# A conditional layer on quarters of TensorE, with a value product between its token tiles, and attention contexts by two groups

## The chip, the cores and the metric

The kernel runs on one core of a Trainium2 chip. The metric is the device time of one execution in microseconds (us), the median over runs; less is better. The engines are called PE or TensorE (matrix products), DVE or VectorE, ACT or ScalarE, POOL or GpSimd, and SP or SyncE, which issues most DMA transfers. PSUM is the memory that TensorE writes its results to, in banks of 128 partitions by 512 float32 values. All matrix products here are in float32, and the trace shows two matmul records for each matmul instruction.

## The reference

The input is 64 batches of 64 tokens by 1024 values. A conditional layer mixes the 64 tokens of each batch with a 64x64 matrix chosen by the batch's condition, then comes attention with 32 heads of 32 values over the 64 tokens of a batch, and a residual. A routed layer and a quantised feed-forward layer follow, with another residual; the change does not touch them.

```python
def _L0_cond_ref(x, condition, weights):
    W = weights[condition]                       # 64 x 64 for each batch
    return jnp.einsum('bct,bcd->bdt', x, W)

def _L0_attn_ref(x, attn_qkvw, attn_qkvb, attn_ow, attn_ob):
    ...
    qkv = x @ attn_qkvw + attn_qkvb              # 1024 -> 3 x 1024
    ...
    scores = jnp.einsum('bhqd,bhkd->bhqk', q, k) * scale
    probs = jax.nn.softmax(scores, axis=-1)
    ctx = jnp.einsum('bhqk,bhkd->bhqd', probs, v)
    ctx = jnp.transpose(ctx, (0, 2, 1, 3)).reshape(B, S, H)
    return ctx @ attn_ow + attn_ob

x = x + _L0_attn_ref(_L0_cond_ref(x, itok_B_0_15, L0_cond_weights), ...)
x = x + _L0_ffn_ref(_L0_cond2_ref(x, itok_B_0_7, ...), ...)
```

## The kernel before

The 4096 tokens are worked in eight blocks (`b`) of 512: four token tiles (`j`) of 128 tokens, each two batches. One function, `attention` (L183), does the conditional layer, the projections to queries, keys and values, and the attention up to the contexts; the contexts go to a DRAM buffer `ctx_d`, and a second stage (out projection, routed layer, feed-forward layer) reads them from there in pairs of tiles. The first two pairs' out projections already run at the end of `attention`.

**Seven products for eight.** Every projection is a 2x2 matrix product by the Strassen-Winograd scheme. The weight matrix has quarters A11, A21, A22, A12 and four sums S1 to S4 (`sums`, L269). The tokens (the output of the conditional layer, transposed, so that rows are features) have quarters B11, B21 (tiles 0 and 1) and B12, B22 (tiles 2 and 3) and four sums T1 to T4 (`t_of`, L369; T4 on L366). A job (L378) makes the products in `ORDER` = 1, 6, 7, 5, 2, 4, 3, on four PSUM banks: products 1 and 2 share bank a, 6 has b, 7 and 4 share c, 5 and 3 share d. Product 1 uses A11 and B11, product 2 uses A12 and B21, product 6 uses S2 and T2. After product 1 ScalarE copies bank a (`p1`, L399); products 6 and 7 leave `u6`, `u7` on VectorE (L402); the other four leave results with `put`. `rows_job` (L416) makes queries (`psq`, into `qT`) and keys (`psk`, into `kbd`, L412/L414) for one of four head groups `c`, with products of 1.72 us; `values_job` (L449) makes values (`psv`, into `vbd`, L468/L470) for one of two column groups `g`, with products of 3.43 us.

**Conditional layer.** `conditional` (L337) copies the 64x64 matrices of the two batches of a tile into the diagonal of a zeroed 128x128 matrix `wbd` (L375; on VectorE for block 0, on GpSimd afterwards). Eight products, one for each tile and feature half `hf`, are four matmuls of 128x128 by 128 columns into one PSUM bank each (L350). Each is copied to B by VectorE (tiles 0 and 2, L356) or ScalarE (tiles 1 and 3, L358). Token tiles and their matrices (`x`, `wg`) are loaded one block ahead (`load_x`).

**Planner.** The order of work is made by a small planner with a clock of its own, `now`. `run(cost, product, rest)` (L598) first does all that is due by `now`, then issues the product, then `behind`, which is the rest (evacuations) of the product before, then one store out of `later`, and then adds `cost` to `now`. Work is put at a time with `at`. A `phase` (L612) takes a list of products ("fills") and puts two groups of attention work into it, one at its beginning and one at half its length.

**A group** is two units of (feature half, token half), 16 score rows. Its `begin` (L573) issues the scores on TensorE (L491), then the contexts of every earlier group that is ready (`contexts`, L566), and then plans the rest: maxima, subtraction and exponential (L503, L504, L507), normalising 3.4 later (L513 to L515), splitting into 16-bit planes (L521), the transposing transfer `phT` on SP's queue (L526), and `pT`, the joined transpose (L533), after another 8. A group is ready for its context when both `pT` are made. `context` (L536) issues 16 matmuls (L543) into a bank of the pool `ps_c`; at once afterwards ScalarE makes two copies with the bias, `co` (L553, pool `p2` with two buffers), and issues each one's store to `ctx_d` from its own queue (L554).

**Pools.** PSUM has four banks "g" for products and the conditional layer, two banks for one tile of scores, and two banks "c" for contexts.

**What the changed parts stand beside.** At the end of a block the fills are `conditional(b+1)`, the first values job of block b+1 and its first query and key jobs. In block 0 the sums S1 to S4 of a weight are made when the weight is first loaded, all four in a row: for `q` and `k` after product 4 of a job (fill 5), for the second value weight in fill 4 of phase 0, and for the second query weight in the first values job. In the last phase of the last block the fills are the out projections of the first two pairs (`poa` to `pod`, L1019), and the last contexts are planned at `now + 41`:

```python
fills += op.pair(0) + op.pair(1)
length = 24
at(now + 41, contexts)
```

Of the kernel before, what the change touches and what calls it, by code (L numbers as in the profile page):

```python
# [20 lines left out]
P = 128  # L21
# [161 lines left out]
def attention(tc, a, x_t, ctx_d, ident, dram, ps_g, KC, PB, NBLK, NCH, HPC, H, C, chores, early, op):  # L183
# [27 lines left out]
    with ExitStack() as ctx, ExitStack() as mid:  # L211
# [5 lines left out]
        pTp = pool(ctx, "pT1", 4, side="right")  # L217
        sm = pool(ctx, "sm1", 3, side="right")
        ps_s = pool(ctx, "ps_s", 1, space=PSUM)
# [49 lines left out]
        def sums(eng, at):  # L269
            eng.tensor_tensor(at("S1"), at("A21"), at("A22"), ALU.add)  # L270
            eng.tensor_tensor(at("S2"), at("S1"), at("A11"), ALU.subtract)
            eng.tensor_tensor(at("S3"), at("A11"), at("A21"), ALU.subtract)
            eng.tensor_tensor(at("S4"), at("A12"), at("S2"), ALU.subtract)
# [4 lines left out]
        def load_qk(b, wh, c, eng=None):  # L278
            t = w_qk[b, wh, c] = wp.tile([P, 7, KQ, P], F32, tag="wqk", name=f"w{wh}_{b}_{c}")
            if b == 0:  # L280
                if (wh, c) == ("q", 0):
                    held(t[:, SLOT["A11"], 0, 0:1], x_next[0][1])
                for key in RAW:
                    nc.sync.dma_start(t[:, SLOT[key], :, :], quarter(key, (0 if wh == "q" else H) + c * P, P))
                def rest():
                    sums(eng or nc.vector, lambda key: t[:, SLOT[key], :, :])
                    nc.gpsimd.dma_start(qk_d[wh, c], t)
                return rest
# [6 lines left out]
        def load_v_raw(g, eng):  # L295
# [9 lines left out]
            def rest():  # L305
                sums(eng, at)
                for slot in range(7):
                    later.append(lambda slot=slot: nc.gpsimd.dma_start(v_d[g][:, slot, :, :], w_v[0, g, slot]))
            return rest
# [3 lines left out]
        first_sums = [load_qk(0, "q", 0), load_qk(0, "k", 0, nc.gpsimd)]  # L313
        nc.sync.dma_start(bqkv, a["qkvb_t"])
        first_sums.append(load_v_raw(0, nc.gpsimd))
# [4 lines left out]
        wbd = []  # L320
        for j in range(PB):
            t = w.tile([P, P], F32, tag=f"wbd{j}", name=f"wbd{j}")
            nc.vector.memset(t, 0.0)
            wbd.append(t)
# [12 lines left out]
        def conditional(b, tiles):  # L337

            def one(hf, j):
                key = f"B{hf + 1}{j // 2 + 1}"  # L340
                box = []

                def product():
                    xt = tiles[j][0]
                    if j % 2 == 0:
                        B[key] = yp.tile([P, KQ, HB], F32, tag=key, name=f"y{key}_{b}")
                    ps = ps_g.tile([P, 4, P], F32, tag="g", name=f"cond_{b}_{j}_{hf}")
                    for q in range(KQ):
                        k = hf * KQ + q
                        nc.tensor.matmul(ps[:, q, :], xt[:, k * P:(k + 1) * P], wbd[j], start=True, stop=True)  # L350
                    box.append(ps)

                def rest():
                    dst = B[key][:, :, (j % 2) * P:(j % 2 + 1) * P]
                    if j % 2 == 0:
                        nc.vector.tensor_copy(dst, box[0])  # L356
                    else:
                        nc.scalar.copy(dst, box[0])  # L358
                    if (hf, j) == (0, 3):
                        t_of("T1", "B12", "B11")  # L360
                    elif (hf, j) == (1, 3):
                        t_of("T2", "B22", "T1")
                        t_of("T3", "B22", "B12")
                    elif (hf, j) == (1, 1):
                        B["T4"] = B["B12"]
                        nc.vector.tensor_tensor(B["T4"], B["B21"], B["T2"], ALU.subtract)  # L366
                return 0.95, product, rest
# [5 lines left out]
            for j, (_, wg) in enumerate(tiles):  # L373
                for r in range(2):
                    (nc.gpsimd if b else nc.vector).tensor_copy(wbd[j][halves[r], halves[r]], wg[halves[r], :])  # L375
            return [one(0, j) for j in range(PB)] + [one(1, j) for j in (2, 3, 0, 1)]

        def job(name, cost, n, matmuls, put, begin=None, done=None):  # L378
# [4 lines left out]
            def one(i):  # L383
                def product():
                    if i == ORDER[0] and begin:
                        begin()
                    bank = BANK[i]
# [1287 lines left out]
```

## Time and profile before

| | us |
|---|---|
| median of 3 runs | 2479.53 |
| the 3 runs | 2477.33, 2479.58, 2479.53 |
| the profiled execution, its own time | 2482.55 |
| its span on the core | 2480.8 |
| of the span, start up to the second product of the first query job | 0.00 to 21.34 |
| attention up to the last block's last phase | 21.34 to 1384.53 |
| last phase of attention, with two pairs' out projections | 1384.53 to 1447.71 |
| second stage | 1447.71 to 2480.80 |

The profile is of one execution. Its span is the time from the first to the last instruction on the core; the time of the execution has some 2 us more around it. Busy times by engine, the chain of work that ended last, groups of equal instructions ("out<-in", count, total and mean time, idle time before them with what ended it) and the records themselves can be read. The mean granted TensorE clock over the span is 0.992 of the full one. What keeps TensorE waiting in the four parts, from the table of its busy time by stretch (columns: stretch in us, then busy us and instructions of PE, PEld, DVE, ACT and POOL, granted clock, DMA share, GB/s):

```profile
0.00:21.34 21.34, 10.53 (x73) 9.98 (x73) 11.93 (x28) 4.38 (x8) 5.02 (x12) 1.00 0.84 262
21.34:1384.53 1363.19, 1354.53 (x9724) 1180.68 (x9727) 831.88 (x1586) 545.63 (x821) 181.76 (x324) 1.00 0.69 210
1384.53:1447.71 63.18, 57.24 (x306) 28.13 (x306) 31.91 (x48) 29.65 (x35) 22.76 (x12) 0.95 0.58 172
1447.71:2480.80 1033.09, 1013.43 (x3136) 485.05 (x3135) 649.13 (x1297) 373.97 (x440) 151.23 (x103) 0.99 0.53 140
```

TensorE is busy for nearly all of the second part, which holds the seven hand-overs from one block to the next.

### The profile page before, as it was taken

How to read it: one execution, taken by the hardware profiler on the slowest of the kernel's cores; microseconds unless marked ns; L12 is line 12 of the kernel's file. 1: busy time of each engine (PE TensorE's matmuls, PEld its weight loads, DVE VectorE, ACT ScalarE, POOL GpSimd, SP SyncE). 2: the span in 40 equal slices, each digit the busy share in tenths (PEclk: the TensorE clock that was granted, in tenths of full speed). 3: DMA queues.
4: the chain of work that ended last, by engine and by line, in shares of the span. 5: the costliest groups of instructions: out<-in, count | busy, mean ns of one | idle time of the engine just before them, and what ended most of it. 6: DMA issues, size and time to landing. Idle time of an engine off the chain costs nothing.

```text
span 2480.8 us, 34182 instructions
## 1 busy us (share of the span) xinstructions
PE 2435.7 (98%) x13232; PEld 1703.8 (69%) x13232; DVE 1524.9 (61%) x2957; ACT 953.6 (38%) x1303; POOL 360.8 (15%) x451
## 2 busy tenths in 40 slices
PE   8999999999999999999999999999999999999996
PEld 7888888888888888888888644444454545454452
DVE  4585585675764755745646623333367777778787
ACT  1243353443443533533534533343423333333333
POOL 5010011011122221110000233334200000000001
PEclk9999999999999999999999999999999999999997
DMA  8795767676677667766646668877744443434343
GB/s 281 262 266 153 225 192 232 191 208 203 205 201 246 206 188 248 201 202 181 171 145 215 187 213 248 271 232 239 227 151 79 87 79 81 85 73 91 71 96 70
DMA packets 417980, 446.76 MB, mean 180 GB/s; under 512 B 299665, under 2 KB 353938, under 8 KB 404114
## 3 DMA queue, kind: packets, MB, share of 16 engines
q1 hardware_dynamic: 387298, 377.90, 52.5%
q0 software_dynamic: 12080, 49.82, 7.6%
q10 hardware_dynamic: 18432, 16.79, 2.0%
q8 instruction: 106, 1.74, 0.3%
q14 instruction: 64, 0.52, 0.1%
HBM read 272.97 MB, written 100.66 MB: 151 GB/s over the span
## 4 chain that ended last, share of the span: by engine, by line
PE 95%; DVE 3%; DMA 1%; issue 1%; ACT 0%; SPq 0%; ACTq 0%; DVEq 0%
PE pska L428 5%; PE psva L455 5%; PE poc L1019 5%; PE pskc L428 4%; PE psvc L455 4%; PE pskd L428 4%; PE psqd L428 4%; PE pbc L1019 4%; PE pba L1019 4%; PE psvd L455 4%; PE psqa L428 4%; PE poa L1019 4%; PE pod L1019 4%; PE pbd L1019 4%; PE psqc L428 4%; PE s L491 3%
## 5 line engine op out<-in xcount | busy, mean ns | idle before, releaser
L533 ACT COPY pT<-phT 128x1024 int16<-128x1024 int16 x128 | 167.2, 1342 | 84.8 <-DMA phT<-ph 84.6
L553 ACT ACTIVATE co<-c,bqkv 128x256 f32<-128x256 f32 x128 | 60.6, 473 | 295.2 <-PE c L543 253.6
L503 DVE TENSOR_REDUCE mx<-s 128x8 f32<-128x512 f32 x128 | 88.3, 690 | 138.0 <-PE s L491 128.4
L521 ACT COPY ph<-prob 128x1024 int16<-128x1024 int16 x128 | 131.4, 1046 | 43.4 <-DVE prob L515 42.7
L414 DVE SCALAR_TENSOR_TENSOR kbd<-pskd,bqkv,psku 32x256 f32<-32x256 f32 x256 | 122.6, 479 | 30.9 <-PE pskd L428 27.2
L507 ACT ACTIVATE prob<-prob 128x512 f32<-128x512 f32 x128 | 78.9, 628 | 154.4 <-DVE prob L504 130.6
L1140 POOL TENSOR_TENSOR xo<-xo,ob 128x1024 f32<-128x1024 f32 x32 | 82.5, 2597 | 375.7 <-DMA xo<-in_x_dram 371.2
L428 PE MATMUL psqa<-yB,wq 128*128 128x256 f32 x512 | 123.5, 384 | 0.0
L428 PE MATMUL pska<-yB,wk 128*128 128x256 f32 x512 | 122.6, 382 | 0.0
L1483 POOL DMA_DIRECT2D out_dram<-y x29 | 25.2, 869 | 653.4 <-DVE y L1475 653.4
L1114 ACT COPY xh<-xo 128x1024 int16<-128x1024 int16 x64 | 64.1, 1040 | 143.8 <-DVE xo L1159 143.4
L455 PE MATMUL psva<-wv,yB 128*128 128x256 f32 x512 | 117.7, 383 | 0.0
L1019 PE MATMUL poa<-woA,cx 128*128 128x512 f32 x256 | 115.3, 593 | 0.0
L1019 PE MATMUL pba<-wtA,x1T 128*128 128x512 f32 x256 | 115.1, 592 | 0.0
L1125 ACT COPY xTo<-xhT 128x1024 int16<-128x1024 int16 x64 | 84.8, 1341 | 64.1 <-DMA xhT<-xh 62.3
L455 PEld LDWEIGHTS psva<-wv,yB 128*128 128x128 f32 x512 | 96.8, 191 | 13.4
L428 PEld LDWEIGHTS pska<-yB,wk 128*128 128x128 f32 x512 | 96.0, 190 | 14.3 <-issue 1.4
L428 PEld LDWEIGHTS psqa<-yB,wq 128*128 128x128 f32 x512 | 95.2, 190 | 13.7 <-issue 0.2
L513 DVE TENSOR_REDUCE den<-prob 128x8 f32<-128x512 f32 x128 | 86.8, 678 | 17.4 <-ACT prob L507 17.2
L504 DVE TENSOR_TENSOR prob<-s,mx 128x512 f32<-128x512 f32 x128 | 88.6, 692 | 9.7 <-DVE mx L503 0.9
L515 DVE TENSOR_TENSOR prob<-prob,den 128x512 f32<-128x512 f32 x128 | 89.8, 702 | 4.4
L412 ACT ACTIVATE kbd<-pska,bqkv 32x256 f32<-32x256 f32 x128 | 59.6, 466 | 79.2 <-PE pska L428 77.6
(243 smaller groups left out, 5138.5 us busy)
## 6 DMA issues: line engine op xcount, KB each, us to landing
wv<-v_d SPq DMA_DIRECT2D x98, 512.0 KB, 3.8
wq<-q_d SPq DMA_DIRECT2D x28, 1792.0 KB, 8.1
wk<-k_d SPq DMA_DIRECT2D x28, 1792.0 KB, 8.2
x<-in_x_dram SPq DMA_DIRECT2D x32, 512.0 KB, 9.8
ctx_d<-co ACTq DMA_DIRECT2D x128, 128.0 KB, 5.6
cx<-ctx_d SPq DMA_DIRECT2D x16, 1024.0 KB, 7.0
xo<-in_x_dram SPq DMA_DIRECT2D x32, 512.0 KB, 5.7
xT_d<-xTo SPq DMA_DIRECT2D x64, 256.0 KB, 4.1
```

The source lines that it names most:

```text
L414: nc.vector.scalar_tensor_tensor(dst, ps, bias, u, ALU.add, ALU.add)
L428: nc.tensor.matmul(ps[:, 0:HB], A[:, SLOT[A_OF[i]], k, :], B[B_OF[i]][:, k, :], start=first and k == 0, stop=k == KQ - 1, skip_group_check ...
L455: nc.tensor.matmul(ps[:, j * VC:(j + 1) * VC], B[B_OF[i]][:, k, j * P:(j + 1) * P], A[:, k, :], start=first and j == 0 and k == 0, stop=k ...
L503: nc.vector.tensor_reduce(mx_v, ps, AX.X, ALU.max)
L504: nc.vector.tensor_tensor(p.rearrange("p (a e) k -> p a e k", a=2), ps, mx_v.unsqueeze(3).to_broadcast([P, 2, HPC, C]), ALU.subtract)
L513: nc.vector.tensor_reduce(den, p, AX.X, ALU.add)
L515: nc.vector.tensor_tensor(p, p, den.unsqueeze(2).to_broadcast([P, n, C]), ALU.mult)
L521: nc.scalar.copy(h, planes(p.rearrange("p n k -> p (n k)")))
L533: nc.scalar.copy(planes(pT.rearrange("p a b q -> p (a b q)")), hT)
L1019: self.nc.tensor.matmul(ps, self.B[self.B_OF[i]][:, k, :], self.A[self.A_OF[i]][:, k, :], start=first and k == 0, stop=k == self.KQ - 1, s ...
L1125: nc.scalar.copy(planes(xT.rearrange("p k q -> p (k q)")), hT)
L1140: nc.gpsimd.tensor_add(s["x"][:, t, :], s["x"][:, t, :], self.ob)
```

## The change

Four things change, all in `attention`.

1. `conditional` has no block-diagonal matrix. Each token tile is one job: for each of eight feature chunks `k`, four matmuls of 64x64 by 64 columns, one on each quarter of TensorE, with the row half `r` (the batch) and the column half `f` (which 64 features). Row half `r` goes to a bank of its own, the first from pool `ps_g`, the second from `ps_c`, the pool of the contexts; a bank takes both feature halves. Four copies of 128x(4x64) evacuate a tile: two on VectorE for the first batch, two on ScalarE for the second. All sums T1 to T4 come after tile 3. The planned cost is 1.2 for each of four tiles instead of 0.95 for each of eight products.
2. The first values job of a block is mixed in: its product 1 stands between tiles 2 and 3. The order of the job is 1, 2, 6, 7, 5, 4, 3, so that product 2, which needs tiles 0 and 1 alone, follows product 1; the copy of bank a comes between them. The first query job of the kernel has the same order.
3. Contexts wait until two groups are ready and are then issued together. The second group's copies and stores are planned 1.7 later. The copies have a pool of their own with four buffers, `pT` has six. Ahead of the contexts a `begin` now issues the rest of the product before. In the last block contexts are planned at `now + 20`, and what is left comes after all fills.
4. The weight sums S1 to S4 are single steps, spread over several products and issued ahead of each: one in each of fills 3 to 6 for the second value weight, two in each of the products 5 and 6 of a job for `q` and `k`, four in fill 4 of the first values job.

```diff
-        pTp = pool(ctx, "pT1", 4, side="right")
+        pTp = pool(ctx, "pT1", 6, side="right")
         sm = pool(ctx, "sm1", 3, side="right")
+        cop = pool(ctx, "co1", 4, side="right")
...
-        def sums(eng, at):
-            eng.tensor_tensor(at("S1"), at("A21"), at("A22"), ALU.add)
-            eng.tensor_tensor(at("S2"), at("S1"), at("A11"), ALU.subtract)
-            eng.tensor_tensor(at("S3"), at("A11"), at("A21"), ALU.subtract)
-            eng.tensor_tensor(at("S4"), at("A12"), at("S2"), ALU.subtract)
+        def sums(eng, at, stored):
+
+            def last():
+                eng.tensor_tensor(at("S4"), at("A12"), at("S2"), ALU.subtract)
+                stored()
+            return [
+                lambda: eng.tensor_tensor(at("S1"), at("A21"), at("A22"), ALU.add),
+                lambda: eng.tensor_tensor(at("S2"), at("S1"), at("A11"), ALU.subtract),
+                lambda: eng.tensor_tensor(at("S3"), at("A11"), at("A21"), ALU.subtract),
+                last,
+            ]
...
-        wbd = []
-        for j in range(PB):
-            t = w.tile([P, P], F32, tag=f"wbd{j}", name=f"wbd{j}")
-            nc.vector.memset(t, 0.0)
-            wbd.append(t)
...
-            def one(hf, j):
-                key = f"B{hf + 1}{j // 2 + 1}"
-                box = []
+
+            def one(j):
+                banks = []
                 def product():
-                    xt = tiles[j][0]
-                    if j % 2 == 0:
-                        B[key] = yp.tile([P, KQ, HB], F32, tag=key, name=f"y{key}_{b}")
-                    ps = ps_g.tile([P, 4, P], F32, tag="g", name=f"cond_{b}_{j}_{hf}")
-                    for q in range(KQ):
-                        k = hf * KQ + q
-                        nc.tensor.matmul(ps[:, q, :], xt[:, k * P:(k + 1) * P], wbd[j], start=True, stop=True)
-                    box.append(ps)
+                    xt, wg = tiles[j]
+                    for r in range(2):
+                        pool_, tag = ((ps_g, "g"), (ps_c, "c"))[r]
+                        banks.append(pool_.tile([P, KC, C], F32, tag=tag, name=f"cond{r}_{b}_{j}"))
+                    for k in range(KC):
+                        for r, f in ((0, 0), (1, 1), (0, 1), (1, 0)):
+                            nc.tensor.matmul(
+                                banks[r][halves[f], k, :], xt[halves[r], k * P + f * C:k * P + (f + 1) * C],
+                                wg[halves[r], :], start=True, stop=True,
+                            )
                 def rest():
-                    dst = B[key][:, :, (j % 2) * P:(j % 2 + 1) * P]
-                    if j % 2 == 0:
-                        nc.vector.tensor_copy(dst, box[0])
-                    else:
-                        nc.scalar.copy(dst, box[0])
-                    if (hf, j) == (0, 3):
+                    for hf in range(2):
+                        key = f"B{hf + 1}{j // 2 + 1}"
+                        if j % 2 == 0:
+                            B[key] = yp.tile([P, KQ, HB], F32, tag=key, name=f"y{key}_{b}")
+                        for r in range(2):
+                            t0 = (j % 2) * P + r * C
+                            src = banks[r][:, hf * KQ:(hf + 1) * KQ, :]
+                            if r == 0:
+                                nc.vector.tensor_copy(B[key][:, :, t0:t0 + C], src)
+                            else:
+                                nc.scalar.copy(B[key][:, :, t0:t0 + C], src)
+                    if j == PB - 1:
                         t_of("T1", "B12", "B11")
-                    elif (hf, j) == (1, 3):
                         t_of("T2", "B22", "T1")
                         t_of("T3", "B22", "B12")
-                    elif (hf, j) == (1, 1):
                         B["T4"] = B["B12"]
                         nc.vector.tensor_tensor(B["T4"], B["B21"], B["T2"], ALU.subtract)
-                return 0.95, product, rest
+                return 1.2, product, rest
             def t_of(key, x, y):
                 B[key] = yp.tile([P, KQ, HB], F32, tag=key, name=f"{key}_{b}")
                 nc.vector.tensor_tensor(B[key], B[x], B[y], ALU.subtract)
-            for j, (_, wg) in enumerate(tiles):
-                for r in range(2):
-                    (nc.gpsimd if b else nc.vector).tensor_copy(wbd[j][halves[r], halves[r]], wg[halves[r], :])
-            return [one(0, j) for j in range(PB)] + [one(1, j) for j in (2, 3, 0, 1)]
-
-        def job(name, cost, n, matmuls, put, begin=None, done=None):
+            return [one(j) for j in range(PB)]
+
+        def job(name, cost, n, matmuls, put, begin=None, done=None, order=ORDER):
             banks, u = {}, {}
             def one(i):
                 def product():
-                    if i == ORDER[0] and begin:
+                    if i == order[0] and begin:
                         begin()
+                    if order[1] == i == 2 and 1 not in u:
+                        behind.pop()()
...
-        def context(b, c, us, pTs):
+        def context(b, c, us, pTs, wait):
             pc = ps_c.tile([P, 2, HB], F32, tag="c", name=f"c_{b}_{c}_{us[0]}")
             for n, (u, pT) in enumerate(zip(us, pTs)):
                 m, t = UNITS[u]
@@ -545,13 +550,20 @@
                                 vbd[c // 2][:, 2 * t + jj, r, m, (2 * c) % 4 + hp, :, :], pT[:, hp, jj, halves[r]],
                                 start=True, stop=True,
                             )
-            for n, u in enumerate(us):
+
+            def copied(n, u):
                 m, t = UNITS[u]
                 ch = m * NP + c
-                co = p2.tile([P, HB], F32, tag="co", name=f"co_{b}_{c}_{u}")
+                co = cop.tile([P, HB], F32, tag="co", name=f"co_{b}_{c}_{u}")
                 nc.scalar.activation(co, pc[:, n, :], AF.Identity, bias=bqkv[:, 2 * KC + ch:2 * KC + ch + 1])
                 nc.scalar.dma_start(ctx_d[2 * b + t][:, ch, :], co)
+
+            for n, u in enumerate(us):
+                if wait:
+                    at(now + wait, lambda n=n, u=u: copied(n, u))
+                else:
+                    copied(n, u)
...
-        def contexts():
-            while waiting and len(waiting[0][3]) == 2:
-                context(*waiting.pop(0))
+        def contexts(least=1):
+            ready = sum(len(pTs) == 2 for *_, pTs in waiting)
+            for n in range(ready if ready >= least else 0):
+                context(*waiting.pop(0), 1.7 * n * (least - 1))
         def group(b, c, us):
             def begin():
                 ps = scores(b, c, us)
-                contexts()
+                if behind:
+                    behind.pop()()
+                contexts(2)
...
+                js = rows_job(b, c, wh, next_load, (1, 2, 6, 7, 5, 4, 3) if n == 0 else ORDER)
                 if b == 0 and n >= 2:
-                    cost, product, rest = js[5]
-
-                    def product_and_sums(product=product):
-                        product()
-                        if pending_sums:
-                            pending_sums.pop(0)()
-                    js[5] = (cost, product_and_sums, rest)
+                    for at_, count in ((5, 2), (6, 2)):
+                        with_sums(js, at_, pending_sums, count)
                 fills += js
             return fills
+
+        def with_sums(fills, i, sums, count):
+            cost, product, rest = fills[i]
+
+            def product_and_sums():
+                for _ in range(min(count, len(sums))):
+                    sums.pop(0)()
+                product()
+            fills[i] = (cost, product_and_sums, rest)
...
+            js = values_job(b, g, next_load, (1, 2, 6, 7, 5, 4, 3) if b and not g else ORDER)
...
+                            for at_ in range(3, 7):
+                                with_sums(fills, at_, v_raw, 1)
                 elif b + 1 < NBLK:
-                    fills += conditional(b + 1, x_next) + v_fill(b + 1, 0) + qk_fill(b + 1, 0)
+                    f, g = conditional(b + 1, x_next), v_fill(b + 1, 0)
+                    fills += f[0:3] + g[0:1] + f[3:4] + g[1:] + qk_fill(b + 1, 0)
                 else:
                     behind.pop()()
                     mid.close()
                     op.open_rest()
                     fills += op.pair(0) + op.pair(1)
                     length = 24
-                    at(now + 41, contexts)
+                    at(now + 20, contexts)
...
-        assert not due and not waiting
+        assert not due
+        contexts()
+        assert not waiting
```

## The prediction

> **What bounds the kernel now.** I read the page's busy table and its chain of waits first, to see whether one engine sets the end.
>
> ```profile
> PE 2435.7 (98%) x13232; PEld 1703.8 (69%) x13232; DVE 1524.9 (61%) x2957; ACT 953.6 (38%) x1303; POOL 360.8 (15%) x451
> ...
> PE 95%; DVE 3%; DMA 1%; issue 1%; ACT 0%; SPq 0%; ACTq 0%; DVEq 0%
> ```
>
> TensorE does: 95% of the chain is its own matmuls. So a microsecond is won where matmuls become fewer or shorter, or where TensorE stands idle, and I priced each edit as TensorE time. The groups by shape show what the edit touches.
>
> ```profile
> L350 PE MATMUL cond<-wbd,x 128*128 128x128 f32 x512 | 62.5, 282 | 12.3 <-DVE wbd L375 9.2 <-DVE yB L356 3.2
> L491 PE MATMUL s<-kbd,qT 64*64 64x128 f32 x2048 | 70.7, 275 | 0.0
> L543 PE MATMUL c<-pT,vbd 128*64 128x64 f32 x2048 | 73.5, 226 | 7.7 <-ACT pT L533 5.9 <-issue 1.8
> ```
>
> The first is the conditional layer: 62.5 us busy, 12.3 of waiting ahead of it. The second already runs on four quarters, the third on two halves. Durations overlap, so the pace comes from starts, below. Then the chain of waits where block 4 hands over to block 5.
>
> ```profile
> 867.99 1.08 PE s L491 x32
> ...
> 872.47 0.69 DVE yB L356
> ...
> 874.56 0.61 DVE yB L356
> ...
> 875.21 2.94 PE cond L350 x24
> 878.16 3.49 PE psva L455 x16
> 881.65 0.43 PE psvb L455 x2
> ```
>
> From the scores to the second values product takes 13.66 us (867.99 to 881.65). The timeline divides it: scores 1.03, one context group 1.08, conditional layer with its stalls 8.06, value product 1 3.49. VectorE's queue (kbd, maxima, copies) holds TensorE up for about 1 us. Seven such boundaries exist. Last, the two long idle stretches that the edit also touches: weight sums in block 0, and the end of attention.
>
> ```profile
> 77.61 1.14 DVE wv L270
> ...
> 79.92 1.23 DVE wv L272
> ...
> 82.31 0.49 DVE qT L414
> ...
> 82.85 2.88 PE psqd L428 x8
> 85.73 4.25 PE psva L455 x16
> ```
>
> ```profile
> 1429.13 7.30 DMA phT<-ph
> ...
> 1436.45 1.35 ACT pT L533
> ...
> 1437.84 1.12 PE c L543 x16
> 1438.97 5.31 PE poc L1019 x8
> ```
>
> In the first, four weight sums in a row hold `qT` on VectorE; TensorE idles 3.03 us, and the 16 matmuls after that take 4.25 where the same product takes 3.45 elsewhere (granted clock 0.50 from 83.80 to 87.20). In the second a context group waits 5.89 us for a transfer; the clock is 0.50 again and `poc` takes 5.31 instead of 3.43.
>
> **The change, part by part (minus is gained).**
>
> *Pace of the quarters.* The trace has no 64x64 matmul with 64 columns. The scores (64x64, 128 columns) run in bursts of four records, one per quarter, 7 ns apart; a burst every 109 ns, so 128 columns stream in 109 ns. The contexts (halves, 64 columns) show two records each 58 ns: 64 columns stream in 58 ns. Four quarters of 64 columns should then give four records per 58 ns. A tile is 32 matmuls of two records: 64 / 4 x 58 ns = 0.93 us; a block 3.72. Before: 32 matmuls at 0.2158 (6.9 us of product time). The other end: no better than the scores' mean of 27.25 ns per record, 1.74 a tile. I take 0.93, since the bursts show starts 7 ns apart. The Trainium skill's page "TensorEngine Tiling (Array Packing)", section Instruction Overhead, speaks against it: some 60 cycles per matmul, and no tiling factor from a dimension that is already small. If that were paid one after the other across quarters, at 2.4 GHz ("TensorE: Matmul & The Clock Gate", Part 1) an estimate is 25 ns a record, 1.6 a tile, and a sum some 15 to 19 us higher; the 7 ns starts speak for its not being so paid, though no row here holds them for long.
>
> *A boundary with two context groups (six of them).* I walked the new order of every engine, in us from the start of the scores. Scores to 1.03, two context groups 2.02 (both banks of the context pool). The second bank of each cond tile now comes from that pool, so cond tile 0 waits for ScalarE's copies of the first group: ScalarE `co` 0.47, issue 0.33, 0.88 from start to start, so the two end at 2.70 and 3.58; tile 0 runs 3.62 to 4.55 (idle 0.57). ScalarE then does an exponential (4.0 to 4.63) and tile 0's two copies (0.354 each, the 128x256 row) to 5.55; tile 1's bank waits for that: 5.6 to 6.53 (idle 1.05). The second group's `co` end near 6.9, tile 2 runs 6.95 to 7.88 (idle 0.42). Value product 1 (3.45) 8.08 to 11.53, 0.2 being the switch that the trace shows after contexts (1.92 instead of 1.73). Tile 3 to 12.56. Product 2 follows at once and needs product 1's copy on ScalarE, behind an exponential, four cond copies, two `pT` (1.36 each) and a `ph` (1.05): 13.75. Idle 1.05. Product 2 13.8 to 17.25; T2 on VectorE is ready at 16.95, so product 6 starts at 17.25. Before, the same work: 13.66 + product 2's 3.45 = 17.11, of which one context group 1.08, so 16.03 without contexts; after, 17.25 - 2.02 = 15.23. Gain 0.80, made of 3.2 less matmul time against about 2.1 more idle and 0.3 of switches. Bounds: no stalls at all, 3.1 more gain; each ScalarE-bound stall doubled, 2.7 less. Six: -4.8. At 0 to 1 no contexts stand there: 15.9 against 16.1, -0.2.
>
> *The cond copies.* 56 POOL copies (234 ns) and block 0's eight on VectorE (190) go; evacuations are halved in size and doubled in number: VectorE 4 x 0.684 becomes 8 x 0.42, ScalarE 4 x 0.585 becomes 8 x 0.354. The extra 0.6 and 0.5 us per block lie under the value products and are in the walk; without that cover they cost 7 x 1.1.
>
> *Start.* Cond starts about 0.5 earlier (no block-diagonal copies) and is done well before 17.8, but VectorE now runs the four `wq` sums, which wait for weights landing at 14.56 and 15.54, ahead of tile 3's copies: sums to 17.3, copies to 18.1, T1 and T2 (1.22 each) to 20.5. The first T2 product starts there, not at 21.34, with product 2 (1.73) already done: -2.6. But TensorE idles some 3.5 us ahead of it, as long as the idle stretches above after which the clock was 0.50 for 3.4 us (1.7 lost). I take -0.9; ends -2.6 and 0.
>
> *Weight sums spread one by one.* `qT` no longer stands behind four 1.2 us adds; the idle 3.03, about 1.1 of queueing behind it and the 0.8 of the slow clock go: -4.9. If each add just delays its own product, half: -2.4.
>
> *Contexts in pairs.* Before 48 single groups and 8 pairs: 48 x 1.08 + 8 x 2.02 = 68.0. After 30 pairs, one triple, one single: 64.7, plus 0.55 wait in the triple (three groups, two banks). -2.8. Delayed second copies lie under products of 1.72 or 3.43.
>
> *Four `co` buffers.* With two, contexts ran into transfers (3.86 us from issue to landing at 558) and TensorE lost 0.8 near 567 and 2.7 between 1070 and 1076. -3.5; ends 0 and -3.5.
>
> *End of attention.* The last groups move behind all eight out products, past the 7.30 us transfer: 5.9 idle and 1.9 of slow clock go, 0.2 comes back. -7.6; ends -4 (the transfer gates another product) and -7.8. The SP order of two wv loads changes with no product waiting near them; the stage from 1447.71 on is untouched.
>
> Sum: -5.0 - 0.9 - 4.9 - 2.8 - 3.5 - 7.6 = -24.7. Profiled: span 2480.8 to 2456.1, execution 2482.55 to 2457.9. That execution was 3.0 above the median 2479.53; against the median, 2454.8, so 2455.
>
> **Rivals.**
> - *Quarters no faster than the scores.* For: no row with a mean under 27 ns a record. Against: the 7 ns starts. Tiles 1.74: +3.24 a boundary, of which 0.4 (tile 2's wait for `co`) and some 0.6 (the product 1 copy) vanish in stalls already counted; +2.2 x 7 = +15.4: 2470. Nothing hidden: 2478.
> - *The idle stretches move, not go.* The end, the sums and `co` together are 16.0; with half kept, 2463; with only the end kept, 2463.4. For: each waits on a transfer or on VectorE, whose work stays. Against: the order puts long products over each wait.
> - *Slower: the cond banks shared with the contexts put ScalarE on the path.* Per boundary TensorE waits for ScalarE four times, about 3.1 us in 17. If ScalarE's queue runs late by more (a `pT` pulled ahead of tile copies costs 1.36 at each of the waits) the clock also drops: 1.7 a window of 3.4 us, as after the two stretches. It decides from 24.7 / 7 = 3.5 us more per boundary; at 2 x 1.36 + 1.7 = 4.4 it gives 2455 + 31 = 2486. For: the walk has four tight waits. Against: ScalarE is busy 38%, and at most 0.5 us of one wait was seen there (VectorE's).
> - *No change:* slow quarters and moved stretches together: 2478.
>
> **How the numbers follow.** Forecast 0.58; slow quarters 0.15; moved stretches 0.10; no change 0.07; slower 0.10. 0.2% (5 us) is about what a measurement of this kernel can tell from no change. Faster: 0.58 + 0.10 + most of 0.15 = 0.81; within: 0.08; slower: 0.11. Time 2455. Low: 3.1 of stalls gone at half the boundaries and the start's other 1.7, about 12: 2443. High: slow quarters plus a little, 2472.
>
> **What would show it.** Right: records of cond 14 to 15 ns apart; stretch from scores to the T2 product near 17.2 at six boundaries, with TensorE waiting for ScalarE's copies; no 5.9 us wait before a context; no `qT` wait at 80; two context groups in 2.02. Wrong: cond records 25 ns or more apart; granted clock 0.50 at boundaries; waits of cond over 6 us per boundary.

## The result and the profile after

The changed kernel takes 2478.03 us (median of 14 executions, 2472.82 to 2482.14); the kernel before, in as many, 2478.55 (2477.15 to 2482.41). The ratio is 0.9997, with a 95% interval of 0.9989 to 1.0005: no difference, where 2455 was forecast. The profiled execution of the changed kernel took 2475.93 us with a span of 2474.1, and was a lucky one, 2.1 under its median; that of the kernel before, 2482.55, was 4.0 over its own. So the two traces differ by 6.7 us where the medians differ by 0.5, and what is read from them is where time went, not how much a typical execution wins.

From the page of the changed kernel, busy time of the engines and the chain that ended last:

```profile
PE 2414.0 (98%) x14730; PEld 1680.8 (68%) x14768; DVE 1543.1 (62%) x2977; ACT 956.0 (39%) x1335; POOL 351.8 (14%) x395
...
PE 93%; DVE 2%; ACT 1%; DMA 1%; issue 1%; ACTq 0%; SPq 0%; DVEq 0%
```

TensorE is busy 21.7 us less than before, yet the span is only 6.7 shorter: most of what was saved became idle time. The conditional layer's group by shape says where (busy, mean ns, then the idle time ahead of it and what ended it), and TensorE's waits say it by releaser (us in total, times, longest):

```profile
L350 PE MATMUL cond<-wg,x 64*64 64x64 f32 x2048 | 42.8, 233 | 32.0 <-issue 14.5 <-DMA wg<-in_condw_dram,idx 8.8 <-ACT yB L366 6.8
```

```profile
PE cond L350 <- issue: 14.5, 6, 3.3
...
PE cond L350 <- ACT yB L366: 6.8, 7, 2.1
...
PE c L548 <- ACT pT L538: 2.5, 1, 2.5
...
PE cond L350 <- ACT co L559: 1.6, 6, 0.3
```

Busy time of cond fell from 62.5 to 42.8, idle time ahead of it rose from 12.3 to 32.0. The largest part, 14.5, is "issue" (12.2 of it at the boundaries between blocks): TensorE waited for nothing that the profile names. The waits that the prediction walked through (for ScalarE's copies) are 6.8 and 1.6. The chain at the boundary from block 3 to 4 shows one such piece; scores begin at 691.21:

```profile
696.08 0.03 ACT yB L366
...
697.51 0.48 ACT co L559
...
698.03 0.57 PE cond L350 x23
698.61 3.15 issue
701.76 1.34 PE cond L350 x39
703.10 4.56 PE psva L460 x16
707.66 1.09 PE cond L350 x64
708.75 3.65 PE psva L460 x16
```

In the middle of tile 2, after 25 of its 64 records, TensorE stops for 3.15 us; the matmuls after the stop read the same token tile and matrices and write the same two banks as those ahead of it. Then value product 1 takes 4.56, as the granted clock is 0.50 from 701.49 to 704.90. In the kernel before, the last 24 records of the conditional layer and value product 1 ran without a break. The end of attention:

```profile
1425.66 3.92 DMA out_dram<-xo
...
1430.51 6.65 DMA phT<-ph
1437.18 1.35 ACT pT L538
...
1438.58 0.99 PE c L548 x16
1439.58 4.95 PE poa L1030 x8
```

The last contexts stand behind all out products now and still wait 2.53 us (1436.05 to 1438.58) for the same chain of store, transposing transfer and `pT`; and the clock falls again (`poa` 4.95).

### The profile page after: what moved, and what is told of

The parts are those of the page before. It is cut to its first block, busy times and chain, and to the rows that moved or that the text cites. A ratio compares the mean times of both kernels' runs of the same rounds, so it can differ in the third digit from the quotient of the medians.

```text
span 2474.1 us, 37277 instructions
## 1 busy us (share of the span) xinstructions
PE 2414.0 (98%) x14730; PEld 1680.8 (68%) x14768; DVE 1543.1 (62%) x2977; ACT 956.0 (39%) x1335; POOL 351.8 (14%) x395
## 4 chain that ended last, share of the span: by engine, by line
PE 93%; DVE 2%; ACT 1%; DMA 1%; issue 1%; ACTq 0%; SPq 0%; DVEq 0%
PE psva L460 5%; PE psvc L460 4%; PE psvd L460 4%; PE pska L433 4%; PE pbc L1030 4%; PE pba L1030 4%; PE psqa L433 4%; PE psqc L433 4%; PE psqd L433 4%; PE pskc L433 4%; PE pbd L1030 4%; PE pskd L433 4%; PE poa L1030 4%; PE poc L1030 4%; PE pod L1030 4%; PE s L496 3%
## 5 line engine op out<-in xcount | busy, mean ns | idle before, releaser
L433 PEld LDWEIGHTS psqa<-yB,wq 128*128 128x128 f32 x512 | 94.5, 190 | 16.3 <-issue 2.8
L475 DVE TENSOR_TENSOR vbd<-psvd,psvu 64x256 f32<-64x256 f32 x128 | 54.0, 422 | 63.3 <-PE psvd L460 61.9
```

The source lines that it names most:

```text
L433: nc.tensor.matmul(ps[:, 0:HB], A[:, SLOT[A_OF[i]], k, :], B[B_OF[i]][:, k, :], start=first and k == 0, stop=k == KQ - 1, skip_group_check ...
```

## The experiments

All times are medians; a ratio is to the kernel before in the same runs. "Unnamed gaps" are pieces of idle TensorE inside the conditional layer or the value product behind it with no named cause; in the changed kernel they are 2.92, 3.15, 1.01, 3.25, 1.90 in cond and 1.06 in the middle of value product 1 (that one is put down to a `pT`, but starts like the others, see below). Two explanations were tried against each other: theory F says that TensorE runs out of instructions, theory S that the shared banks and ScalarE's queue hold it up.

### Half the instructions, and the contexts moved: e1 to e4

e1 puts a tile on two row halves, e2 moves the contexts of a boundary, e3 is both, e4 shifts the instruction stream:

```diff
 # e1, e3
-for r, f in ((0, 0), (1, 1), (0, 1), (1, 0)):
-    nc.tensor.matmul(banks[r][halves[f], k, :], xt[halves[r], k * P + f * C:k * P + (f + 1) * C], wg[halves[r], :], ...)
+for r in range(2):
+    nc.tensor.matmul(banks[r][:, k, :], xt[halves[r], k * P:(k + 1) * P], wg[halves[r], :], ...)
 # e2, e3
-contexts(2)
+if c == NP - 1 and b + 1 < NBLK and us[0] == 0:
+    at(now + 11.5, lambda: contexts(2))
+else:
+    contexts(2)
 # e4
-for k in range(KC):
+for k in list(range(KC)) * (2 if (b, j) == (0, 0) else 1):
```

> The conditional layer of the changed kernel on two row halves of TensorE (64 rows by 128 columns) instead of four quarters: 16 matmuls a tile instead of 32, so half the instructions; banks, copies, order and waits stay. In the changed kernel TensorE stands idle in the middle of a cond tile for 2.92, 3.15, 1.01, 3.25 and 1.90 us at five of seven boundaries (12.2 in all), with nothing named that it waits for. Theory F (TensorE's own instruction stream: 16 KB instruction transfers land late where matmuls are short and dense): the gaps vanish or leave under 2 us in all, and no slow clock follows them. A tile costs 0.93 us if the weight load of 128 columns keeps up, and then the time is some 12 to 16 us less than the changed kernel's 2478, about 2464; or up to 1.73, and then it is 2478 to 2481 in spite of the gaps' going. Theory S (the bank shared with the contexts, and ScalarE's queue): banks and queue are the same, so the gaps of about 3 us stay at the same boundaries, 10 us or more in all.

> The changed kernel with the two context groups of each boundary issued after value product 2 instead of before the cond tiles. This takes 128 instructions out of the dense stretch and leaves the cond banks free at its start. Theory F: the gap in tile 2 or 3 shrinks (below 1 us at most boundaries, 5 us or less in all), as at the first boundary, which has no contexts and shows no such gap; the 0.26 wait for the copies of contexts goes too. About 12 us less than 2478, near 2466. Theory S (banks and ScalarE's queue): the same waits go, so much the same time; the two differ in whether a stretch with idle TensorE remains without a named wait. If neither holds and slow clock alone is the cause: no change.

> Both edits together: row halves and the contexts after value product 2. Theory F: no gap without a named wait at any boundary. If a tile on halves takes 0.93 us, 2460 to 2464, the best of the three; if it takes 1.73 us, 7 x 3.2 = 22 us of matmul time come back and it is no better than 2475. Theory S: like e2, as the number of instructions does not matter.

> The changed kernel with the matmuls of block 0's first tile issued twice, that is 128 more TensorE instructions (half of a 16 KB transfer of 256) at the start and about 1 us more work there; nothing else. Theory F: the boundaries stand otherwise against the transfers, so the gaps move: the one at the boundary 2 to 3, which had none, gets one of 1 to 3 us, and at least two of 2.92, 3.15 and 3.25 fall below 2. Theory S: the gaps stay as they were at each boundary, within 0.5 us.

| | time | ratio (95%) | unnamed gaps at the boundaries | clock at 0.50 there |
|---|---|---|---|---|
| changed kernel | 2478.03 | 0.9997 (0.9989 to 1.0005) | 13.3 us | 13.7 us |
| e1 row halves | 2505.92 | 1.0105 (1.0090 to 1.0119) | none | 54.6 us |
| e2 late contexts | 2473.39 | 0.9973 (0.9963 to 0.9983) | 5.6 us | 17.1 us |
| e3 both | 2477.59 | 0.9989 (0.9981 to 0.9998) | none | 10.2 us |
| e4 shifted | 2484.85, one run | | 16.3 us | 20.5 us |

The kernel before had 2479.55 in these runs. In e1 and e3 the unnamed gaps are gone, in e1 with banks, copies and order as they were: this is what theory F said and theory S excluded. What was wrong is e1's time. A tile on halves takes 1.73 us, and then the clock fell at all six boundaries with contexts; theory F had expected no slow clock (last section). In e2 the gaps shrink to less than half, but a named wait of 1.9 to 2.2 us now stands ahead of a tile at each of the six boundaries with contexts: its bank waits for ScalarE's copies, which stand behind an exponential. So 5 to 6 us of the expected 12 came (4.6 between the medians, 5.6 when each is set against the kernel before in its own runs). In e4 the boundary that had no gap inside cond got one, of 3.45 us where 1 to 3 was expected; but the others kept 2.79, 3.40 and 2.50, where two were expected under 2. The stops did move against the work (at the boundary from block 1 to 2 from 6.6 to 7.9 us behind the scores' start), and the sum rose by 3 us: the size of the loss depends on where the instruction buffers end.

What they end at can be counted in the traces. TensorE's instructions come by transfers of 16,384 bytes; the page lists them as an instruction queue, before and after:

```profile
q8 instruction: 106, 1.74, 0.3%
```

```profile
q8 instruction: 118, 1.93, 0.3%
```

(Packets, MB, share.) The first is the kernel before with 26,464 LDWEIGHTS and matmul records, the second the changed kernel with 29,498: some 250 a transfer, so 256 with what is not recorded. Counting every TensorE instruction up to the start of each gap:

```
changed kernel, gaps:        354.21  530.79  698.61  871.62  1043.23  1216.65
instructions before it:        5825    8897   11713   14529    17601    20417
modulo 256:                     193     193     193     193      193      193
transfer landed at:          355.67  530.55  700.39  871.25  1045.23  1216.98
gap ends:                    357.13  531.85  701.76  872.63  1046.48  1218.56
```

Every unnamed gap begins at the same place of a 256-instruction buffer and ends 1.25 to 1.6 us after a transfer has landed; the named wait of 2.12 at 179.91 begins at 2877, which is 61. e2, e4, e8, e10 and e12 give the same 193 for each of theirs. So TensorE ran out of instructions. Not every unnamed stop is of this kind: in the last phase e1, e2, e3, e10 and e11 stop once for 1.2 to 3.2 us ahead of `pob`, at 12, 213, 213, 15 and 0 of a buffer, and the cause of these is open. After a gap, transfers start 3.5 to 4.3 us apart (699.43 and 703.40; 870.37, 874.33 and 878.65), which is some 60 to 70 instructions a microsecond. A product of 1.73 us uses 16 of them, scores 64 in 1.03 us, two context groups 128 in 2.02, a tile on quarters 128 in 0.96, and three of these come in a row. That the transfers set the pace is inferred from these counts and from e1, e3 and e8; no run changed the transfers themselves.

### Terms of the prediction alone: e5 to e7

Each is the kernel before with one part of the change: the context copies in a pool of four buffers (e5); the weight sums as single steps, spread (e6); `at(now + 20, contexts)` and a last `contexts()` after all fills (e7).

> The kernel before with four instead of two buffers for the context copies, nothing else. The prediction's term: 3.5 us less, as the idle time near 567 and 1072 of the profiled execution was put down to the two buffers. Rival: those idle pieces were chance of that one execution (the second lies inside the contexts beside an instruction transfer that lands at 1072.67, and it was the slowest of the executions of the kernel before): then no difference, within 1.5 us of the kernel before, and no idle time named co in either.

> The kernel before with the weight sums as single steps spread over products, as the change has them, nothing else. The prediction's term: 4.9 us less (idle 3.03 and 1.1 of queueing and 0.8 of slow clock near 80 us go). Rival: the sums only delay what follows, half is kept, 2.4 less; or the time comes back by the end, 0.

> The kernel before with the last contexts planned at 20 and behind all out products instead of 41, nothing else (contexts still one group at a time). The prediction's term: 7.6 less. What the profile of the changed kernel shows: the wait shrinks from 5.94 to 2.53 and the slow clock stays, as the transposing transfer itself comes 3.7 us later against the last scores: then 3 to 4 less. If ScalarE's and SP's queues absorb it: 0.

| | time | ratio (95%) | predicted term |
|---|---|---|---|
| e5 | 2481.73 | 0.9998 (0.9988 to 1.0007) | -3.5 |
| e6 | 2478.56 | 0.9986 (0.9977 to 0.9996), -3.5 us | -4.9 |
| e7 | 2472.70 | 0.9960 (0.9946 to 0.9974), -9.9 us | -7.6 |

The kernel before had 2481.97 in these runs. e5 is nothing: the gaps near 1072 are still there (0.34, 0.33, 0.37, 0.36), inside contexts and beside a transfer of instructions that lands at 1072.87. They had been read as a wait for buffers. (The smaller piece near 567, 0.58 in the trace of before and put down to `vbd`, is not in e5's trace.) The rival's "chance" fits only the longest piece, 1.04 in the trace of before, since e5, e6 and e7 all have the short ones. In all four traces they stand some ten instructions apart around instruction 15,360, which is 60 x 256; what makes them short and several is open. The terms of e6 and e7 lie inside their intervals (for e7 6.5 to 13.4 us less), and e7 brings more than the half that the changed kernel kept. In its profile the last contexts hardly wait:

```profile
1426.66 0.70 DVE ou L1155
...
1428.48 3.94 DMA out_dram<-xo
...
1433.36 7.36 DMA phT<-ph
1440.74 1.39 ACT pT L533
1442.17 0.69 PE c L543 x16
1442.85 3.63 PE poa L1021 x8
```

Against the last scores (1403.69), the store begins 24.8 us later here, in the changed kernel 28.1 (1425.66 against 1397.59). Two things stand ahead of it there. On ScalarE two context copies and their issues run from 1412.2 to 1413.9, ahead of the output copies `xh`, since pairing had moved that group out of the scores' begin. On VectorE, `xo` and the four `To` (L1040 to L1043) stand ahead of the maxima, since a `begin` now issues the rest of the product before: the first maxima start 10.0 us behind the start of the last scores instead of 1.2, and the last `xo` 17.1 instead of 14.9.

### Parts undone, and better versions: e8 to e12

e8 issues tiles 0 and 1 among the products of the last key job, which is done in the order 1, 2, 6, 7, 5, 4, 3 so that their B buffers are free:

```diff
+if c + 2 == NP and b + 1 < NBLK:
+    early_tiles = conditional(b + 1, x_next)
+    fills[13:13] = early_tiles[1:2]
+    fills[11:11] = early_tiles[0:1]
...
-fills += f[0:3] + g[0:1] + f[3:4] + g[1:] + qk_fill(b + 1, 0)
+fills += f[2:3] + g[0:1] + f[3:4] + g[1:] + qk_fill(b + 1, 0)
...
+    at(now + 9.2, lambda: contexts(2))
```

e9 is e8 with `contexts(1)` in the last phase. e10 is the changed kernel with `contexts()` for `contexts(2)`; e11 the changed kernel with the block-diagonal conditional layer of before, its eight products two to a tile in the same places; e12 the kernel before with the change's conditional layer alone.

> The changed kernel with cond tiles 0 and 1 of the next block issued among the last key job's products of this block (order 1, 2, 6, 7, tile 0, 5, 4, tile 1, 3), tiles 2 and 3 around value product 1 as before, and the contexts of the boundary after value product 2. The same matmuls, thinned out. Theory F: with at most 128 dense instructions between longer products no gap without a named wait over 1 us at most boundaries, no slow clock there; the named waits of tiles 1 and 2 (1.0 to 2.2 us) go too. From the scores to product 6 some 13.5 us, with two tiles (2.3) outside it, 15.8 against 17.2 to 21.2 of the changed kernel: 2478 - 7 x 3.4 = 2454, range 2450 to 2462. If instead ScalarE's queue is what decides, the copy of product 1 behind the exponentials holds product 2 up by some 3 us and it is near 2470.

> e8 with the contexts of the last phase of the last block issued as soon as one group is ready, so that the group c_7_2_2 is done at the second scores and its two copies on ScalarE stand before, not inside, the chain that leads to the last transposing transfer. In e8 the end still waits 2.43 us for that transfer and then runs 3.4 us at the slow clock; e7, which has the single groups, waited 0.21. Theory (ScalarE's queue ahead of the output copy delays the transfer): 3 to 4 us less than e8, so about 1.2% under the kernel before. Rival (the transfer is set by SP's queue and the store before it): no change from e8.

> The changed kernel with contexts issued as soon as one group is ready, as in the kernel before; all else of the change stays. At the boundaries one group instead of two stands ahead of the tiles, 64 TensorE instructions (LDWEIGHTS and matmuls) fewer. Theory F: the gaps without a named wait fall from 12.2 to about half in all, and tile 0 waits less for copies; against that some 20 groups cost 0.14 us more; near 2474. Theory S: the waits named co shrink by 2 x 0.88 us at each boundary at most, and the gaps stay: 2476.

> The changed kernel with the conditional layer of the kernel before (block-diagonal 128x128 matrices, eight products of four matmuls, banks of ps_g only), in the order of tiles, value product 1 between tiles 2 and 3 and the rest of the change kept. Tells what the quarters are worth in the place they have. Theory F: no gap without a named wait at boundaries and no slow clock there; cond takes 6.9 instead of 3.7 us a block; 22 us more matmul time against 12 of gaps, 5 of slow clock and 6 of waits for the shared bank: about the same as the changed kernel, 2473 to 2481. If the gaps had another cause they stay, and it is 2490 or more.

> The kernel before with the conditional layer of the change alone: quarters, four tiles in a row, one bank from the pool of the contexts, T sums after tile 3; value products in the old order behind it, single contexts. Theory F: 512 dense TensorE instructions in a row, so gaps of 2 to 4 us without a named wait at most of the seven boundaries; the 22 us of shorter matmuls are given back by these and by slow clock: 2472 to 2484. Theory S: only named waits (copies of tile 0 and 1, 1 to 2 us), 2465.

| | time | ratio (95%) | unnamed gaps at the boundaries | clock at 0.50 there |
|---|---|---|---|---|
| e8 early tiles | 2454.83 | 0.9894 (0.9877 to 0.9910) | 1.1 us | none |
| e9 early, single at the end | 2451.03 | 0.9891 (0.9874 to 0.9907) | 0.4 us | none |
| e10 single contexts | 2485.09 | 1.0026 (1.0016 to 1.0036) | 20.7 us | 23.9 us |
| e11 old conditional | 2461.88 | 0.9937 (0.9920 to 0.9954) | none | none |
| e12 quarters alone | 2502.65 | 1.0097 (1.0080 to 1.0114) | 19.3 us | 37.5 us |

The kernel before had 2481.97 beside e8 and 2478.38 beside the others. e8 has the same matmuls as the changed kernel, only thinned out and with the boundary's contexts behind value product 2, and is 1.06% faster than the kernel before; TensorE's waits in it:

```profile
PE psva L460 <- ACT psvp L404: 3.1, 2, 1.5
...
PE cond L350 <- issue: 2.3, 2, 1.2
```

e9 beats both kernels as well; that it beats e8 by 3 to 4 us was expected and isn't shown, the ratios are equal. Its last contexts still wait 2.10 us (2.43 in e8): the store begins 27.5 us behind the last scores instead of 29.2, as the copies no longer stand ahead of it, while the order on VectorE stayed.

e11 was expected level with the changed kernel and is 0.6% faster, some 15 us. At its boundaries TensorE goes from the scores to product 6 in 17.2 us at four of six and 17.4 and 17.9 at the others, with no idle piece over 0.4. TensorE's rows of the boundary from block 4 to 5, first e11, then the changed kernel, where it is the best of the six with 17.23 us (865.13 to 882.36):

```profile
863.04 5.62 PE L355 MATMUL cond<-wbd,x 128*128 128x128 f32 x48
868.50 3.62 PE L460 MATMUL psva<-wv,yB 128*128 128x256 f32 x16
871.95 1.95 PE L355 MATMUL cond<-wbd,x 128*128 128x128 f32 x16
873.74 3.63 PE L460 MATMUL psva<-wv,yB 128*128 128x256 f32 x16
```

```profile
868.77 1.16 PE L350 MATMUL cond<-wg,x 64*64 64x64 f32 x64 [0.26 <-ACT co L559]
870.71 0.91 PE L350 MATMUL cond<-wg,x 64*64 64x64 f32 x42 [0.78 <-ACT yB L366]
872.63 1.50 PE L350 MATMUL cond<-wg,x 64*64 64x64 f32 x84 [1.01 <-issue]
```

e11 has 17.2 us of work there; the changed kernel has about 15.2 of work and 2.06 of idle time, half of it the unnamed gap. So the quarters' shorter matmuls turned into idle time; without the gap this boundary would take some 16.2 (an estimate, 17.23 - 1.01). That the quarters can pay where instructions keep up is seen in e8: 12.5 to 14.3 us at these boundaries, plus some 2.7 for the two early tiles (four key products and two tiles take 9.58 there, four products alone 6.9), so 15.2 at the best three against 17.2.

e12 shows the quarters alone with four tiles in a row: 24 us lost, more than expected, with gaps of 19.3 us and the clock at 0.50 for 37.5 us. e10 was expected at 2474 and missed: with one context group ahead the gaps are larger, not smaller. Contexts use 63 instructions a microsecond, about the rate of supply, so leaving a group out gives the supply 1 us less before the tiles and no lead; that reading was made afterwards and not tried.

## Why the prediction was wrong, step by step

- **Pace of the quarters: right.** 64 records of a tile start within 0.94 us (707.6 to 708.5), 15.0 ns each; 14.5 was taken.
- **A boundary with two context groups: the step that failed.** The walk gave 17.25 us to product 6. Measured: 20.39, 17.44, 21.03, 17.23, 21.23, 18.34. It had no row for TensorE's own instruction stream, and every one of the six has such a gap, 13.3 us in all, with the slow clock behind the three longest: 12.2 us more than the walk in sum. Two of the waits it named are there (0.26 for `co`, 0.78 for tile 0's copies, by the profile's account). The one of 1.05 ahead of product 2 is not: TensorE goes from tile 3 into product 2 without idle time at all six. So 17.44 and 17.23, where the gap was only 1.0, are near 17.25 partly by luck: a gap stands in the place of a wait that did not come.
- **Rivals.** The slow clock at boundaries and the price of 1.7 a window were right in the third rival (21.03 against 17.23, less 2.14 for the longer gap, leaves 1.66), but ScalarE was the wrong cause. The first rival (pace) was wrong; in the second, the end kept half, as said.
- **Start:** -0.9 taken, -0.6 at the first scores. **Sums:** -4.9 taken, -3.5 alone, with the term inside the interval.
- **Four `co` buffers: misread.** The pieces of idle time near 1072 stand around the end of an instruction buffer, not at a wait for buffers of `co`, and the long one was in that execution alone; e5 gives 0 where 3.5 was taken.
- **End:** -7.6 taken, -9.9 alone, -3.7 in the changed kernel's trace (41.9 us from the last scores to the third pair, plus 1.5 of slow clock, against 47.1), with the context copies ahead of the output copies on ScalarE and the later maxima on VectorE. e9 took the copies away, which brought the store 1.7 us nearer to the scores; the order on VectorE was not undone in any run, so how much it cost is not shown.
- **Sum.** In the two traces, with the other terms as forecast: -24.7 + 12.2 (boundaries) + 0.35 (the first) + 3.9 (end) + 0.3 (start) = -8.0, measured -6.7. In the medians there are 6 us more to explain: 4.0 and 2.1 are where the profiled executions stood among the others. Executions of the changed kernel spread over 9.3 us; that gaps vary so much between them is likely, but not shown.
- **Net.** The change is two effects that cancel: all but the quarters gains 0.63% (e11), some 16 us; the quarters in this place, four dense tiles with one product between them, lose that again.

## What to carry to other kernels

Ask of small matmuls not only how long they stream, but how many instructions a microsecond they use: where TensorE idles with no named wait, count its instructions to the start of each gap modulo the size of a transfer. Thin a dense stretch with long products when making its matmuls shorter: the same quarters lost some 15 us in the changed kernel (against e11) and won in e8. Idle pieces seen in one profile of one execution are not to be put down to a cause that lies merely beside them.

## What the runs showed of the hardware

The granted clock changes on a grid of 3.41 us, and a window with little idle time can be enough for it to fall. Table by stretch of e1 (stretch, then busy us of PE, PEld, DVE, ACT, POOL, then granted clock, DMA share, GB/s) and of the changed kernel:

```profile
358.53:361.94 3.41, 2.68 (x48) 2.54 (x48) 1.96 (x4) 1.95 (x5) 0.00 (x0) 1.00 0.94 324
361.94:372.18 10.24, 10.24 (x59) 9.05 (x58) 4.57 (x11) 5.21 (x9) 0.00 (x0) 0.50 0.17 58
```

```profile
868.74:872.15 3.41, 2.07 (x106) 1.79 (x107) 2.31 (x5) 2.12 (x5) 0.00 (x0) 1.00 0.98 347
872.15:875.57 3.42, 2.94 (x91) 2.72 (x91) 2.33 (x6) 2.57 (x6) 0.00 (x0) 1.00 0.62 220
```

In e1 0.73 us of idle time, in a window of cond on halves, was followed by 10.2 us at 0.50; in the changed kernel 1.34 us in a window of quarters was not. Idle time alone does not tell the two apart. How much of the array was in use does better in these runs: each record's share of the array times its columns, at 0.85 ns a column (109 ns for 128, from the scores), as a share of the window. That is 0.35 for the window of e1 above (0.30 to 0.35 for its six drops) and 0.42 for the one of the changed kernel, where the five drops up to the end of attention followed windows of 0.05 to 0.25. Over all traces, from 20 us to the end of attention, no drop followed a window above 0.42; below that some windows had none (down to 0.32 in e1), so it is no sharp rule. The Trainium skill, "TensorE: Matmul & The Clock Gate", section "Why this matters for your kernels", asks for no idle gaps of more than about 3 us; the runs here show drops after less.

A tile on row halves costs 1.73 us against 0.96 on quarters, though both stream 64 columns; its weights have 128 columns instead of 64, and a weight load takes 240 ns on the mean instead of 145. That the loads set the pace is not shown. And the page "TensorEngine Tiling (Array Packing)", section Instruction Overhead, has about 60 cycles a matmul; the prediction's estimate from it, 25 ns a record if paid in a row, is not what quarters do: 15.0 ns were measured.
